# Order of GpSimd's work around the second routing of a mixture-of-experts kernel: weights spread first, gathers of two units ahead of the fifth single's adding, columns ahead of the sixth's

## The chip, the cores and the metric

The kernel runs on one core of a Trainium2 chip. The metric is the device time of one execution in microseconds (us), the median of several. The core has five engines that run side by side and meet at semaphores: TensorE (PE; its weight loads are PEld), VectorE (DVE), ScalarE (ACT), GpSimd (POOL) and SyncE (SP). DMAs are issued by SyncE, ScalarE and GpSimd; all of them run on the same 16 DMA engines. An engine works through its own instructions in their written order: an instruction that waits holds up all that stand behind it on that engine.

## The reference, cut to what matters

`x` is 64 x 64 tokens of 256 numbers. Every token goes to 2 of 8 experts, each of three layers (256 to 512, 512 to 512, 512 to 256), and the weighted sum is added to the token:

```
xn   = rms_w * x * rsqrt(mean(x*x) + 1e-6)
gate = xn @ wg_W + wg_b + (cond @ gg_W + gg_b)
w, i = top_k(softmax(gate), 2)               # cw: the two weights at their experts, else 0
h1   = relu(x @ W1[e] + b1[e])
h2   = relu(h1 @ W2[e] + b2[e])
out  = x + sum over e of cw[e] * (h2 @ W3[e] + b3[e])
```

## The kernel before

Tokens are sorted to their experts, so that only chosen pairs are computed: 4096 tokens x 2 = 8192 pairs. A tile is up to 128 pairs of one expert. For each tile GpSimd does three kinds of DMA with an index per row: a gather of the tokens' rows of x (line 859, into `xg`, `big` or `xgE`), a gather of their routing weights, the "columns" (line 859 too, into `cg`), and at the end an adding of the tile's results onto the rows of `out` in memory (line 1347). An adding reads rows and writes them back, so each unit's adding waits until that of the unit before has landed.

There are two routings. The first covers a quarter of the tokens (`pA`) and fills seven single tiles, units 0 to 6, of which each has an expert of its own: "the fifth single" is unit 4, "the sixth" unit 5. Their indices are `idxA`, their weights lie in memory in `cwdA`. While TensorE works on the singles, the second routing (`pB`, the generator `rest()`, advanced step by step by `routing()`) sorts all that is left: VectorE makes lists, TensorE turns them into a table (line 628), VectorE makes the indices `idxR` of the table (lines 787 and 788). The routing weights of all tokens are worked out by `weights()` on VectorE (lines 433 to 435) and put in place and stored in memory, in `cwdR`, by `spread()` on GpSimd (lines 439 to 442).

From unit 7 on (`F` = 7) a unit is up to four tiles of one expert, and the layers are computed by seven half-size products instead of eight (the classes `Fast` for the first two layers and `Wide` for the third). Unit 7's rows are gathered into `big` and turned by TensorE (line 932). The rows of unit 8 are gathered into `xgE`, and of later units into the two by turns; SyncE regroups them through memory (`stow`, line 898, and `shuffle`, line 905), and VectorE transposes them in blocks (line 914). The copies of x to `out` for the other three quarters of the tokens (`fill`, line 1427) are issued by SyncE too, two before unit 6 and two in unit 6 behind the shuffle of unit 8.

The order is written out by hand (`manual_schedule`): each engine's queue holds its instructions as the program is written. The main program around the change is:

- `head_step(u)` for units 0 to 5: layer 1 of u, layer 3 of u - 1, `give(u - 1)` (VectorE scales the results, line 1346, GpSimd adds them, line 1347), a step of the routing, layer 2 of u. `head_step(5)` gives unit 4, and in it the last step of `rest()` makes the index and gathers unit 7 (`gather_unit(F)`).
- `step(6)`: gathers unit 8, copies and spreads the weights (line 1444 and `spread`), then layer 1 of unit 6, layer 3 and `give` of unit 5, then `gather_cw(7)`, the four gathers of unit 7's columns.
- `step_fast(7)`: gathers unit 9's rows and unit 8's columns; VectorE copies each tile's own column out of `cg` (`scales`, line 1007), then sums products of layer 2 (`c11`, line 1157; in the next step `c22`, line 1163, and `c12`, line 1160); ScalarE scales the biases by the columns (line 1024). `give(6)` comes here.

At a switch in the program ("tail") the later units take one of several written orders, by the data. Each DMA of GpSimd also takes one of eight semaphores in turn, and does not start before the DMA that had the same semaphore, the eighth before it, has landed.

## Time and profile before

| | |
|---|---|
| median of 3 runs | 455.2 us (455.04 to 457.39) |
| the profiled execution | 455.39 us, of it the span 453.7 us |
| busy: TensorE, VectorE, ScalarE, GpSimd | 442.7, 359.2, 259.9, 272.6 us |
| mean granted clock of TensorE | 0.988 |
| moved by DMA | 71.72 MB, 158 GB/s on average |

A row of the timeline gives the start in us from the start of the span, the length, the engine, the line of the kernel, the operation, what it writes and reads (without buffer numbers), how many instructions are merged, and in brackets how long the engine stood idle before and what the wait was put down to. Starts of matmuls are pipelined and their ends are modelled, so the time from start to start is surer than the length. A row of the stretches gives the stretch, its length, the busy time (and number) of PE, PEld, DVE, ACT and POOL, the granted clock of TensorE as a share of full speed, the mean busy share of the DMA engines, and GB/s. "DMA to landing" is the time from the issue of a DMA to its end, least, median and most.

### The profile page before, as it was taken

What the parts mean: (1) busy time and instruction counts of PE and PEld (TensorE: products, weight loads), DVE (VectorE), ACT (ScalarE), POOL (GpSimd) and SP (SyncE); (2) the same over time, 40 slices, a digit from 0 to 9 for tenths busy, and PEclk for the clock granted to TensorE, in tenths of its full rate; (3) what the DMA queues carried; (4) which work ended last, traced back from release to release, by engine and by line L of the source; (5) the groups of instructions that cost most, each with busy time, mean ns of one, the idle gap of its engine ahead of it and who ended that gap; (6) DMA issues with size and microseconds to landing.
All of it is one profiled execution on the core that took longest, in us unless ns stands there. A gap on an engine that the chain in (4) does not pass through costs nothing.

```text
span 453.7 us, 9412 instructions
## 1 busy us (share of the span) xinstructions
PE 442.7 (98%) x3058; PEld 413.8 (91%) x3058; DVE 359.2 (79%) x974; ACT 259.9 (57%) x626; POOL 272.6 (60%) x238
## 2 busy tenths in 40 slices
PE   9999999997999999999999999999999999999994
PEld 7689999786989888989999899999999999999984
DVE  5789996458797979888899788778878888779851
ACT  6865643436464466555565565664764755666642
POOL 5356323868785755648375764864863875766242
PEclk9899999998999999999999999999999999999998
DMA  8799999396776655554655563563663665455213
GB/s 292 296 355 380 367 376 346 104 290 172 190 133 165 110 142 114 116 111 93 167 90 102 124 131 79 130 146 73 124 130 83 111 148 118 115 116 104 23 20 38
DMA packets 71567, 71.72 MB, mean 158 GB/s; under 512 B 35215, under 2 KB 60914, under 8 KB 71124
## 3 DMA queue, kind: packets, MB, share of 16 engines
q1 hardware_dynamic: 48944, 42.51, 29.9%
q0 software_dynamic: 14960, 17.50, 23.3%
q10 hardware_dynamic: 7604, 11.02, 7.7%
q8 instruction: 26, 0.43, 0.4%
q14 instruction: 33, 0.27, 0.2%
HBM read 55.42 MB, written 20.25 MB: 167 GB/s over the span
## 4 chain that ended last, share of the span: by engine, by line
PE 82%; DMA 5%; issue 4%; POOL 4%; DVE 3%; POOLq 1%; ACT 0%; SPq 0%; DVEq 0%; ACTq 0%
PE pb L1145 51%; PE pb L1247 18%; PE pb L1046 4%; PE pb L1315 3%; PE pb L1036 2%; DMA big<-in_x_dram 2%; POOL out_dram L1347 2%; DMA w3r<-in_L_cond_W_dram 1%; DMA cg<-cwdR,idxR 1%; PE pb L258 1%; POOL xgE L859 1%; POOL big L859 1%; DVE xT L914 0%; PE pb L628 0%; DVE big L1122 0%
## 5 line engine op out<-in xcount | busy, mean ns | idle before, releaser
L1347 POOL DMA_INDIRECT out_dram<-ys,idxR x58 | 100.2, 1728 | 89.5 <-DVE ys L1346 75.2
L1145 PE MATMUL pb<-hid,big 128*128 128x256 f32 (+7 forms) x456 | 84.5, 329 | 0.0
L1166 ACT ACTIVATE hid<-hid,bb 128x256 f32<-128x256 f32 (+12 forms) x154 | 73.5, 527 | 14.0 <-DVE hid L1160 13.5
L859 POOL DMA_INDIRECT cg<-cwdR,idxR x60 | 65.2, 1087 | 20.4 <-issue 18.1
L1145 PEld LDWEIGHTS pb<-hid,big 128*128 128x128 f32 x456 | 71.2, 191 | 4.4 <-ACT hid L1166 0.8
L1154 ACT COPY big<-pb 128x512 f32<-128x512 f32 (+7 forms) x57 | 27.5, 482 | 67.6 <-PE pb L1145 50.5
L1145 PE MATMUL pb<-mixB,big 128*128 128x256 f32 (+7 forms) x304 | 58.1, 335 | 2.5 <-DVE hid L1163 2.5
L1145 PE MATMUL pb<-hotA,big 128*128 128x256 f32 (+7 forms) x304 | 56.2, 328 | 0.0
L1145 PEld LDWEIGHTS pb<-mixB,big 128*128 128x128 f32 x304 | 49.4, 194 | 6.5 <-DVE hid L1163 2.8
L1145 PEld LDWEIGHTS pb<-hotA,big 128*128 128x128 f32 x304 | 47.1, 191 | 2.3
L1145 PE MATMUL pb<-mixX,iotx 128*128 128x256 f32 (+7 forms) x228 | 47.0, 329 | 0.0
L859 POOL DMA_INDIRECT xgE<-in_x_dram,idxR x33 | 35.7, 1083 | 10.1 <-issue 8.8
L1154 ACT COPY q1s<-pb 128x512 f32<-128x512 f32 (+7 forms) x57 | 27.2, 476 | 22.1 <-PE pb L1145 20.8
L1145 PEld LDWEIGHTS pb<-mixX,iotx 128*128 128x128 f32 x228 | 36.7, 191 | 3.1 <-issue 0.8
L1268 DVE TENSOR_TENSOR ys<-pb,big 128x256 f32<-128x256 f32 (+1 forms) x54 | 19.2, 355 | 24.8 <-PE pb L1247 19.0
L859 POOL DMA_INDIRECT big<-in_x_dram,idxR x27 | 29.2, 1080 | 8.2 <-issue 7.6
L1024 ACT ACTIVATE bc<-b_sb,cw 128x256 f32 x60 | 26.6, 499 | 9.7 <-DVE cw L1007 8.9
L914 DVE STREAM_TRANSPOSE xT<-gTs 128x256 f32<-128x256 f32 x56 | 30.0, 644 | 2.8 <-DMA gTs<-scr 2.8
L1145 PE MATMUL pb<-xT,w1r 128*128 128x256 f32 (+7 forms) x152 | 31.3, 329 | 0.0
L1166 ACT ACTIVATE hid<-pb,bb 128x256 f32<-128x256 f32 (+7 forms) x76 | 27.7, 417 | 2.4 <-PE pb L1145 1.8
L1256 ACT COPY big<-pb 128x256 f32<-128x256 f32 (+1 forms) x54 | 17.0, 314 | 20.8 <-PE pb L1247 20.7
L1247 PE MATMUL pb<-w3r,hid 128*128 128x128 f32 x216 | 27.2, 275 | 0.0
(347 smaller groups left out, 920.3 us busy)
## 6 DMA issues: line engine op xcount, KB each, us to landing
w2a<-in_L_cond_W_dram SPq DMA_DIRECT2D x8, 1024.0 KB, 11.2
w3r<-in_L_cond_W_dram ACTq DMA_DIRECT2D x11, 512.0 KB, 4.3
w1r<-in_L_cond_W_dram SPq DMA_DIRECT2D x10, 512.0 KB, 11.1
w1r<-in_L_cond_W_dram ACTq DMA_DIRECT2D x10, 512.0 KB, 3.8
w3r<-in_L_cond_W_dram SPq DMA_DIRECT2D x9, 512.0 KB, 11.5
gTs<-scr SPq DMA_DIRECT2D x8, 512.0 KB, 4.4
out_dram<-in_x_dram SPq DMA_DIRECT2D x4, 768.0 KB, 8.3
scr<-xgE SPq DMA_DIRECT2D x6, 512.0 KB, 4.0
```

Source lines behind the costliest of these rows:

```text
L859: return nc.gpsimd.indirect_dma_start(out=dst, out_offset=None, in_=src, in_offset=bass.IndirectOffsetOnAxis(ap=index(b), axis=0), bounds_ ...
L914: V.transpose(xT[:, :, s0 + k, :].rearrange("p c (b k) -> p k c b", b=SQ), shs[:, s0 + k].rearrange("p k (a c) -> p k c a", a=SQ),)
L1024: nc.scalar.mul(bc, b3e, cw)
L1046: nc.tensor.matmul(ph, lhsT=w2[:, m, ts(n, P)], rhs=hid[0][:, m, 0:BT], start=(m == 0), stop=(m == MC - 1))
L1145: nc.tensor.matmul(bank[:, ts(n, self.w)], lhsT=w[:, c, ts(n, P)], rhs=x[:, c], start=new and n == 0 and c == 0, stop=n == HB - 1 and c == ...
L1154: nc.scalar.copy(self.q[(1, 6, 5).index(k)], self.tall(self.X if k == 5 else self.U))
L1166: nc.scalar.activation(out, src, AF.Relu, bias=ww[self.u][1][:, self.l, n : n + 1])
L1247: nc.tensor.matmul(bank[:, ts(j, H // 2)], lhsT=a[:, c, ts(j, P)], rhs=b[:, c], start=new and j == 0 and c == 0, stop=j == self.n - 1 and ...
L1256: nc.scalar.copy(self.q[(1, 6, 5).index(k)], self.X if k == 5 else self.U)
L1268: V.tensor_tensor(self.y(j, i), src, self.q[q].rearrange("p (k h) -> p k h", k=self.n), ALU.add)
L1315: nc.tensor.matmul(sums(u, k)[0 : cols.stop - cols.start], lhsT=hid[1][:, n, cols], rhs=w3[:, n, :], start=(i == 0), stop=(i == MC - 1),)
L1347: add = nc.gpsimd.indirect_dma_start(out=orows, out_offset=bass.IndirectOffsetOnAxis(ap=index(b)[0:n], axis=0), in_=y[0:n], in_offset=None ...
```

## The change

Three things move on GpSimd, and nothing else does: the orders of the other engines stay as they were.

The spread of the weights (the copy of the first part's weights, three operations and the DMA to `cwdR`) leaves `step(6)` and stands in `rest()` right behind `weights()`, ahead of the index and of the gathers of unit 7. The addings of units 4 and 5 leave `give`, which now only notes them in `owed`; `pay()` issues them one by one: unit 4's in `step(6)` behind the gathers of unit 8, unit 5's behind the columns of unit 7.

```diff
         pB.weights()
+        nc.gpsimd.tensor_copy(cw8B[:, 0:NA, :], pA.cw8)
+        pB.spread(cwdR, cw8B, 0)
         yield
         table()
...
         if u not in given:
             given[u] = 0
-            adds.append([])
+            if not F - 3 <= u < F - 1:
+                adds.append([])
...
             given[u] += 1
+            if F - 3 <= u < F - 1:
+                owed.append((b, y[0:n]))
+            else:
+                add_rows(b, y[0:n])
...
+    owed = []
+
+    def pay():
+        adds.append([])
+        add_rows(*owed.pop(0))
+
+    def add_rows(b, y):
...
         if u == F - 1:
             gather_unit(F + 1)
-            nc.gpsimd.tensor_copy(cw8B[:, 0:NA, :], pA.cw8)
-            pB.spread(cwdR, cw8B, 0)
+            pay()
             layer1(u)
...
             give(u - 1)
             gather_cw(F)
+            pay()
```

`add_rows` holds the adding as it stood in `give`, with the same waits.

The queue of GpSimd where the fifth single's adding stood, before. The names are those of the program: `out_0_dram<-ys_193` are the addings of units 2 and 3, `out_0_dram<-xg_1_208` that of unit 4, `big_89` the gathers of unit 7, `xgE_184` those of unit 8, `cw8B_138` the weights being spread:

```order
L1347 DMA out_0_dram<-ys_193,idxA_130 4096x256 x2
L1347 DMA out_0_dram<-xg_1_208,idxA_130 4096x256
L859 DMA big_89<-in_x_dram,idxR_131 128x256 x4
L859 DMA xgE_184<-in_x_dram,idxR_131 128x256 x4
L1444 COPY cw8B_138<-cw8A_162 128x64
L439 TENSOR_TENSOR cw8B_138<-ohB_173,denB_169 128x192
L440 TENSOR_TENSOR wB_172<-ohB_173,d2B_170 128x192
L441 TENSOR_TENSOR cw8B_138<-cw8B_138,wB_172 128x192
L442 DMA cwdR_58<-cw8B_138 128x256
```

The same place of the same queue now (line numbers are those of the changed file, in which 859 is 861, 1347 is 1366 and 1444 is 785):

```order
L1366 DMA out_0_dram<-ys_193,idxA_130 4096x256 x2
L785 COPY cw8B_138<-cw8A_162 128x64
L439 TENSOR_TENSOR cw8B_138<-ohB_173,denB_169 128x192
L440 TENSOR_TENSOR wB_172<-ohB_173,d2B_170 128x192
L441 TENSOR_TENSOR cw8B_138<-cw8B_138,wB_172 128x192
L442 DMA cwdR_58<-cw8B_138 128x256
L861 DMA big_89<-in_x_dram,idxR_131 128x256 x4
L861 DMA xgE_184<-in_x_dram,idxR_131 128x256 x4
L1366 DMA out_0_dram<-xg_1_208,idxA_130 4096x256
```

The spread has moved ahead of the eight gathers, and unit 4's adding from ahead of them to behind them.

Right behind this in GpSimd's queue, before. `xg_2_209` and `xg_0_207` hold the results of units 5 and 6, the two times four gathers into `cg_185` are the columns of units 7 and 8, and those into `big_89` the rows of unit 9:

```order
L1347 DMA out_0_dram<-xg_2_209,idxA_130 4096x256
L859 DMA cg_185<-cwdR_58,idxR_131 128x8 x4
L859 DMA big_89<-in_x_dram,idxR_131 128x256 x4
L859 DMA cg_185<-cwdR_58,idxR_131 128x8 x4
L1347 DMA out_0_dram<-xg_0_207,idxA_130 4096x256
```

And now:

```order
L861 DMA cg_185<-cwdR_58,idxR_131 128x8 x4
L1366 DMA out_0_dram<-xg_2_209,idxA_130 4096x256
L861 DMA big_89<-in_x_dram,idxR_131 128x256 x4
L861 DMA cg_185<-cwdR_58,idxR_131 128x8 x4
L1366 DMA out_0_dram<-xg_0_207,idxA_130 4096x256
```

Unit 5's adding has moved behind unit 7's columns; the rest stands as it did.

## The prediction

> **What bounds the kernel now.** I read the page first, for the engine that is nearly always busy.

> ```profile
> span 453.7 us, 9412 instructions
> PE 442.7 (98%) x3058; PEld 413.8 (91%) x3058; DVE 359.2 (79%) x974; ACT 259.9 (57%) x626; POOL 272.6 (60%) x238
> ```

> TensorE is the bound, so GpSimd's order is worth only what it costs TensorE in waits. The stretches of the trace (length, then the busy time of each engine, the granted clock, the DMA share) say where those are.

> ```profile
> 102.00:104.00 2.00, 0.52 (x3) 0.12 (x1) 0.86 (x4) 1.15 (x3) 1.59 (x2) 1.00 1.04 355
> 104.00:106.00 2.00, 1.13 (x3) 0.95 (x4) 2.00 (x6) 1.84 (x5) 1.50 (x2) 0.69 0.46 140
> 106.00:108.00 2.00, 2.00 (x6) 1.57 (x5) 1.96 (x4) 1.24 (x3) 1.70 (x2) 0.50 0.31 59
> 108.00:110.00 2.00, 2.00 (x10) 1.77 (x9) 1.74 (x4) 1.23 (x3) 1.50 (x2) 0.96 0.85 207
> ...
> 110.00:150.00 40.00, 40.00 (x241) 36.70 (x241) 33.13 (x73) 20.91 (x43) 29.52 (x23) 1.00 0.65 151
> 150.00:240.00 90.00, 89.85 (x539) 82.10 (x538) 76.30 (x175) 51.24 (x109) 54.41 (x43) 1.00 0.56 124
> 262.00:435.00 173.00, 173.00 (x1298) 170.34 (x1296) 141.38 (x382) 107.60 (x276) 107.01 (x80) 1.00 0.50 106
> ```

> The hole is at 102 to 105 us, and behind it the clock is 0.69 and 0.50. From 110 us on TensorE is full, so time won before that should come through to the end. The two timelines of the hole, TensorE's and then VectorE's (start, length, idle before it):

> ```profile
> 99.77 1.89 PE L1145 MATMUL pb<-hid,big 128*128 128x256 f32 x8
> 101.50 1.03 PE L1145 MATMUL pb<-mixX,iotx 128*128 128x256 f32 x4
> 104.87 3.60 PE L1145 MATMUL pb<-mixB,big 128*128 128x256 f32 x8 [2.35 <-DVE hid L1163]
> 108.31 1.03 PE L1145 MATMUL pb<-xT,w1r 128*128 128x256 f32 x4
> ```

> ```profile
> 97.27 2.11 DVE L914 STREAM_TRANSPOSE xT<-gTs 128x256 f32<-128x256 f32 x4 [2.79 <-DMA gTs<-scr]
> 99.41 0.43 DVE L1128 TENSOR_TENSOR mixX<-xT 128x256 f32<-128x256 f32 x1
> ...
> 103.45 0.15 DVE L1007 COPY cw<-cg 128x1 f32 x1 [0.18 <-DMA cg<-cwdR,idxR]
> 103.53 0.69 DVE L1157 TENSOR_TENSOR hid<-pb,big 128x512 f32<-128x512 f32 x1
> 104.14 0.68 DVE L1163 TENSOR_TENSOR hid<-pb,big 128x512 f32<-128x512 f32 x1
> ```

> TensorE waits for unit 7's sum at L1163, which needs nothing from the routing weights; it merely stands on VectorE behind the four copies of L1007, which wait for the gathered columns cg. Those come late from GpSimd:

> ```profile
> 66.88 1.56 POOL L1347 DMA_INDIRECT out_dram<-ys,idxA  x1 [7.18 <-DVE big L777]
> 74.35 1.55 POOL L1347 DMA_INDIRECT out_dram<-xg,idxA  x1 [5.91 <-DMA w3r<-in_L_cond_W_dram]
> 76.20 1.08 POOL L859 DMA_INDIRECT big<-in_x_dram,idxR  x1 [0.30 <-issue]
> ...
> 85.54 1.16 POOL L859 DMA_INDIRECT xgE<-in_x_dram,idxR  x1 [0.30 <-issue]
> 86.71 0.24 POOL L1444 COPY cw8B<-cw8A 128x64 f32<-128x64 f32 x1
> ...
> 89.17 0.63 POOL L442 DMA_DIRECT2D cwdR<-cw8B  x1 [0.30 <-POOL cw8B L441]
> 90.10 1.95 POOL L1347 DMA_INDIRECT out_dram<-xg,idxA  x1 [0.31 <-issue]
> 93.69 1.07 POOL L859 DMA_INDIRECT cg<-cwdR,idxR  x1 [1.64 <-DMA cwdR<-cw8B]
> ...
> 97.69 1.00 POOL L859 DMA_INDIRECT cg<-cwdR,idxR  x1 [0.30 <-issue]
> ```

> The adding at 74.35 stood 5.91 us until the adding before it had landed. (The row names a load of weights, but in the code it waits only for its own rows, which VectorE had written before, and for that adding; the releaser in the row is inferred.) Everything behind it stood too, though the indices were there:

> ```profile
> 67.65 0.18 DVE L435 TENSOR_TENSOR d2B<-d2B,denB 128x24 f32<-128x24 f32 x1
> ...
> 69.98 0.23 DVE L788 SCALAR_TENSOR_TENSOR idxR<-pb,sa 128x70 int32<-128x70 f32 x1
> ```

> **The change part by part.** No engine gets other work; nothing is added or removed but places in GpSimd's queue.

> *Spread first.* Its last input is ready at 67.65 + 0.18 = 67.83 us, the adding ahead of it leaves GpSimd at 66.88 + 1.56 = 68.44. Four operations and one DMA took from 86.70 to 89.80, 3.10 us; now they end at 71.54. They fill the wait of 5.91 us, so they cost TensorE nothing; without that cover they would cost the gathers 3.10 us.

> *Gathers of two units ahead of the fifth adding.* The first starts at 71.54 + 0.31 = 71.85 instead of 76.20, 4.35 earlier (index ready at 70.21). Eight take 86.70 - 76.20 = 10.50 us and end at 82.35. TensorE wants unit 7's rows here:

> ```profile
> 80.29 0.92 PE L932 MATMUL pb<-ident,big 128*128 128x128 f32 x4
> ...
> 82.46 0.27 PE L932 MATMUL pb<-ident,big 128*128 128x128 f32 x1
> 83.06 0.62 PE L932 MATMUL pb<-ident,big 128*128 128x128 f32 x3 [0.33 <-DMA big<-in_x_dram,idxR]
> 83.52 1.03 PE L1145 MATMUL pb<-xT,w1r 128*128 128x256 f32 x4
> ```

> The second set of four would end at 82.46 + 0.92 = 83.38 instead of 83.06 + 0.62 = 83.68: 0.30 us to win. Landing times bound the risk (columns; rows; the plain copies x to out; and one row of the DMA issues, its last column the landing):

> ```profile
> DMA to landing us min/median/max: 2.2/4.2/7.5
> ...
> DMA to landing us min/median/max: 2.8/4.5/6.2
> ...
> DMA to landing us min/median/max: 7.1/8.3/9.6
> ...
> w3r<-in_L_cond_W_dram SPq DMA_DIRECT2D x3, 512.0 KB, 10.9
> ```

> The second gather, now at 71.85 + 1.30 = 73.15, must land by 80.29, and the fourth, at 75.75, by about 82.5. Even the slowest gather of rows, 6.2 us, gives 79.35 and 81.95. The eight semaphores hold nobody: the seventh gather, at 71.85 + 6 x 1.30 = 79.65, waits for the adding of 66.88, which had landed by 74.35, and the eighth, 1.30 later, for the weights' write, which leaves GpSimd at 71.54 and needed 93.69 - 89.80 = 3.89 us to land. I take no wait; the ends are 2.8 and 7.5 us, and at 7.5 TensorE loses 0.4 and keeps the second wait.

> [...]

> ```profile
> 73.77 0.69 DVE L1092 COPY big<-w2a 128x1024 f32 x1
> 74.37 0.43 DVE L1094 COPY big<-w2a 128x512 f32 x1
> ```

> The gather at 76.20, beside other work of VectorE, took 1.08 us, 0.08 over the 1.00 at 97.69; no gather stands beside these copies in the trace. I take 0.1 for all of them; the far end is a gather held for both copies, 1.12 us, which would use up the 0.94 us of room (80.29 - 79.35). [...]

> *Fifth adding, then columns, then sixth adding.* The fifth goes at 82.35 + 0.31 = 82.66 and leaves at 84.21. The columns start at 84.52, not 93.69: 9.17 us earlier, the fourth at 88.52. Slowest landing, 7.5: 96.0 us. The sixth adding waits for the fifth to land, 84.21 + 5.91 = 90.12, about where it was (90.10); only unit 9's gathers queue behind it, at some 92.4 instead of 99.00 us. Nobody on TensorE waits for an adding here.

> *SyncE's queue.* Its order stays; the regrouping of unit 8's rows waits for their gathers, so with it everything behind moves up by 4.35 us, these too:

> ```profile
> 92.95 1.16 SPq L1427 DMA_DIRECT2D out_dram<-in_x_dram x2
> ```

> They start at 88.60, the crowd that delayed the columns goes with them, and three of the four columns are now issued before it.

> *What is late next.* L914 can start at 97.27 - 4.35 = 92.92 if VectorE is free; even where it stood, the copies come at 99.9 and are done at 100.5, and the sums end 1.29 us later (103.53 to 104.82), at 101.8. TensorE asks for L1163 when the four matmuls of 101.50 are through: 101.50 + 0.87 = 102.37 (the same form runs 0.86 or 0.87 from start to start). So the columns may land as late as 100.9, 4.9 us after their slowest case, and the wait goes wholly: 104.87 - 102.37 = 2.50 us.

> *The clock.* The eight matmuls behind the hole take 108.31 - 104.87 = 3.44 us, eight of the same size before it 101.50 - 99.77 = 1.73. Without the hole I expect the clock to stay at 1.00: 1.71 us. [...]

> **The sum:** 0.30 + 2.50 + 1.71 = 4.51 us. The profiled execution took 455.39 us (its span 453.7 and 1.7 around it), 0.2 over the median of 455.2. I forecast 455.2 - 4.5 = 450.7 us; the 0.1 us of the gathers comes out of their room.

> **The rivals.** *The crowd moves with the columns.* They land with the last of the copies, now also delayed by the fifth adding and unit 9's gathers; a wait of up to 1 us stays on L1163. For it: those gathers now run into the crowd. Against it: the copies' slowest landing gives 88.60 + 9.6 = 98.2, below 100.9. It gives 451.7, or 453.4 if the clock falls too.

> *The clock falls anyway*, for another reason than the hole: 455.2 - 2.8 = 452.4. Against it: it is 1.00 before the hole and after 110. [...]

> *Given back later.* A faster TensorE meets another wait, say the switch into the tail near 150 us, where 0.15 us idle stand now. Up to 455.2; the full rows from 110 us speak against it.

> *It does nothing:* the columns' landing hangs on the crowd alone and ends at 103.4 again: 455.2.

> *Slower: unit 7's rows come late.* They are issued into the fullest DMA stretch, behind an adding and the weights' write. Every us after 80.29 is one of TensorE's, and once it waits as long as the hole did the clock costs another 1.71. With the gains of 4.21 left, it is even from a wait of 2.50, a landing 9.6 us after the issue, as of the slowest copy. At the 10.9 of the w3r loads the wait is 3.76: 3.76 + 1.71 - 4.21 = 1.26, 456.5 us; slower by 0.5% from a landing in 12 us.

> **How the numbers follow.** Forecast 0.74, crowd 0.10, clock 0.05, given back 0.05, nothing 0.03, late rows 0.03. The forecast's own range is 449.8 to 451.5 (wait ends of 0.4 and 0.3, and the spread of the executions); the clock case and the better half of the crowd bring it to 452.9, with some 0.85 inside. A measurement of this kernel can tell about 0.5%, 2.3 us, from no change. Below 452.9: forecast, clock, half the crowd, a part of given back, 0.86; slower 0.03; the rest 0.11.

> **What would show it.** Right: spread at 68 to 72 on GpSimd, first gather near 72, columns near 84.5, L1007 without a wait, TensorE without idle time at 102 and the clock 1.00 there, the same lengths from 110 on. Wrong: idle time before L932 near 80, a wait of L1163 or L914 that TensorE feels, a low clock without a hole, or new holes after 110.

## The result, and the profile after

The changed kernel takes 449.21 us (median of 6 runs, 449.06 to 449.97), the kernel before beside it 455.14 (6 runs, 454.83 to 457.39): a ratio of 0.9864, 95% interval 0.9844 to 0.9885, or 5.2 to 7.1 us faster. The forecast was 450.7, with a range from 449.8: the direction was right, and the gain was larger than the range allowed. The profiled execution took 449.12 us, 6.27 less than that of before. In two groups of experiments the kernel before itself took 476 to 477 us, with waits between the engines all over the program, and nothing is concluded from those kernels.

The page after, its first lines:

```profile
span 447.3 us, 9411 instructions
PE 438.9 (98%) x3058; PEld 411.8 (92%) x3058; DVE 359.5 (80%) x974; ACT 259.1 (58%) x626; POOL 273.8 (61%) x238
```

Every engine's busy time is within 1.2 us of before's, but for TensorE's and its weight loads', 3.8 and 2.0 us less. The stretches where the hole was, and one of 173 us behind the switch into the tail:

```profile
100.00:102.00 2.00, 2.00 (x11) 1.77 (x10) 1.91 (x4) 1.17 (x3) 1.70 (x2) 1.00 0.53 175
102.00:104.00 2.00, 2.00 (x11) 1.77 (x10) 1.38 (x4) 1.40 (x4) 1.39 (x3) 1.00 0.06 9
...
255.00:428.00 173.00, 173.00 (x1296) 170.30 (x1296) 141.30 (x382) 107.56 (x276) 107.37 (x80) 1.00 0.51 106
```

No hole, a clock of 1.00, and the stretch of 173 us that ran full before runs full again. GpSimd's timeline after:

```profile
66.25 1.57 POOL L1366 DMA_INDIRECT out_dram<-ys,idxA  x1 [7.29 <-DVE big L778]
67.25 0.82 POOL L785 COPY cw8B<-cw8A 128x64 f32<-128x64 f32 x1
67.46 1.24 POOL L439 TENSOR_TENSOR cw8B<-ohB,denB 128x192 f32<-128x192 f32 x1
...
70.29 0.65 POOL L442 DMA_DIRECT2D cwdR<-cw8B  x1 [0.30 <-POOL cw8B L441]
71.25 1.10 POOL L861 DMA_INDIRECT big<-in_x_dram,idxR  x1 [0.30 <-DMA w3r<-in_L_cond_W_dram]
...
73.97 1.42 POOL L861 DMA_INDIRECT big<-in_x_dram,idxR  x1 [0.30 <-issue]
75.69 1.52 POOL L861 DMA_INDIRECT big<-in_x_dram,idxR  x1 [0.30 <-issue]
...
82.78 1.61 POOL L1366 DMA_INDIRECT out_dram<-xg,idxA  x1 [0.30 <-issue]
84.69 1.04 POOL L861 DMA_INDIRECT cg<-cwdR,idxR  x1 [0.31 <-issue]
...
90.00 2.10 POOL L1366 DMA_INDIRECT out_dram<-xg,idxA  x1 [0.30 <-issue]
92.40 1.26 POOL L861 DMA_INDIRECT big<-in_x_dram,idxR  x1 [0.30 <-PE pb L1147]
```

The wait of 5.91 us is filled, the columns start at 84.69 instead of 93.69. VectorE's timeline where L914 (now 916), the copies (now 1009) and L1163 (now 1165) stand:

```profile
92.73 2.09 DVE L916 STREAM_TRANSPOSE xT<-gTs 128x256 f32<-128x256 f32 x4
...
95.20 0.21 DVE L1009 COPY cw<-cg 128x1 f32 x2
95.59 0.28 DVE L1009 COPY cw<-cg 128x1 f32 x2 [0.18 <-issue]
...
97.45 0.69 DVE L1165 TENSOR_TENSOR hid<-pb,big 128x512 f32<-128x512 f32 x1 [0.95 <-PE pb L1147]
```

The copies wait for no DMA now, and at L1165 it is VectorE that waits for TensorE. TensorE's timeline at unit 7's rows and at the former hole:

```profile
79.45 0.64 PE L934 MATMUL pb<-ident,big 128*128 128x128 f32 x4
79.93 0.60 PE L1317 MATMUL pb<-w3r,hid 128*128 128x256 f32 x2
...
81.34 0.63 PE L934 MATMUL pb<-ident,big 128*128 128x128 f32 x4
81.80 1.03 PE L1147 MATMUL pb<-xT,w1r 128*128 128x256 f32 x4
...
99.77 1.03 PE L1147 MATMUL pb<-mixX,iotx 128*128 128x256 f32 x4
100.64 1.89 PE L1147 MATMUL pb<-mixB,big 128*128 128x256 f32 x8
102.36 0.81 PE L1147 MATMUL pb<-xT,w1r 128*128 128x256 f32 x3
```

Set against before's rows, by the start of the same instructions on TensorE, the 6.4 us of difference between the spans come at four places:

| place | before minus after, us |
|---|---|
| start of the kernel, ahead of everything changed | 0.79 |
| unit 7's rows: four matmuls, layer work, four matmuls | 0.93 |
| hole (2.50) and half clock (3.44 - 1.72) | 4.23 |
| short waits for ScalarE near 157 us | 0.39 |

The first and the last are not the change's. The first is a clock that was low in before's profiled execution and not in the changed kernel's; before, then after, the stretch from 20 us:

```profile
20.00:22.00 2.00, 2.00 (x10) 1.32 (x7) 1.20 (x7) 1.19 (x3) 1.90 (x4) 0.50 0.51 146
```

```profile
20.00:22.00 2.00, 1.64 (x16) 1.39 (x13) 1.83 (x8) 1.07 (x2) 1.89 (x4) 1.00 0.68 144
```

Nothing before 66 us was changed, and the low clock turns up at this place in three later profiles that hold the change's own parts (the third part left out, the hole put back, one of the two repeats of the change; granted clocks over the whole span 0.993, 0.994 and 0.993) and not in the others (0.995 to 0.999, and 0.993 with the sixth adding alone, where it fell behind the hole). The last is not the change's either. The stretch of products around it took TensorE 10.55 us in before and 10.16 in the changed kernel, but 9.89 to 10.25 in the nine later profiles, and 9.89 to 10.14 in those of them that are before with the sixth adding moved or with products in the hole. So 5.2 of the 6.3 us belong to the change: 0.93 + 4.23 = 5.16.

### The profile page after: what moved, and what is told of

The parts are those of the page before. It is cut to its first block, busy times and chain, and to the rows that moved or that the text cites. A ratio compares the mean times of both kernels' runs of the same rounds, so it can differ in the third digit from the quotient of the medians.

```text
span 447.3 us, 9411 instructions
## 1 busy us (share of the span) xinstructions
PE 438.9 (98%) x3058; PEld 411.8 (92%) x3058; DVE 359.5 (80%) x974; ACT 259.1 (58%) x626; POOL 273.8 (61%) x238
## 4 chain that ended last, share of the span: by engine, by line
PE 91%; DMA 3%; DVE 2%; issue 1%; POOLq 1%; POOL 1%; SPq 0%; DVEq 0%
PE pb L1147 57%; PE pb L1249 19%; PE pb L1048 6%; PE pb L1317 3%; PE pb L1038 3%; DMA big<-in_x_dram 2%; PE pb L628 1%; POOL out_dram L1366 1%; DMA xg<-in_x_dram,idxA 1%; DVE xT L916 0%; PE pb L924 0%; POOLq L1693 0%; PE pb L1294 0%; POOLq L1782 0%; PE pb L258 0%
## 5 line engine op out<-in xcount | busy, mean ns | idle before, releaser
L1366 POOL DMA_INDIRECT out_dram<-ys,idxR x58 | 98.7, 1701 | 90.4 <-DVE ys L1349 75.8
L1147 PE MATMUL pb<-hid,big 128*128 128x256 f32 (+7 forms) x456 | 84.5, 329 | 0.0
L1147 PEld LDWEIGHTS pb<-hid,big 128*128 128x128 f32 x456 | 71.2, 191 | 4.4 <-ACT hid L1168 0.8
L1147 PE MATMUL pb<-mixB,big 128*128 128x256 f32 (+7 forms) x304 | 56.3, 328 | 0.2 <-DVE hid L1165 0.2
L1147 PE MATMUL pb<-hotA,big 128*128 128x256 f32 (+7 forms) x304 | 56.2, 328 | 0.0
L1147 PEld LDWEIGHTS pb<-mixB,big 128*128 128x128 f32 x304 | 48.4, 191 | 3.4 <-ACT bc L1026 0.5
L1147 PEld LDWEIGHTS pb<-hotA,big 128*128 128x128 f32 x304 | 47.1, 191 | 2.3
L1147 PE MATMUL pb<-mixX,iotx 128*128 128x256 f32 (+7 forms) x228 | 46.9, 329 | 0.0
L861 POOL DMA_INDIRECT xgE<-in_x_dram,idxR x33 | 37.2, 1127 | 10.1 <-issue 8.5
L1147 PEld LDWEIGHTS pb<-mixX,iotx 128*128 128x128 f32 x228 | 36.8, 191 | 2.9 <-issue 0.8
L861 POOL DMA_INDIRECT big<-in_x_dram,idxR x27 | 30.5, 1129 | 8.2 <-issue 7.3
L1147 PE MATMUL pb<-xT,w1r 128*128 128x256 f32 (+7 forms) x152 | 31.3, 329 | 0.0
## 6 DMA issues: line engine op xcount, KB each, us to landing
w3r<-in_L_cond_W_dram ACTq DMA_DIRECT2D x11, 512.0 KB, 3.8
w1r<-in_L_cond_W_dram SPq DMA_DIRECT2D x10, 512.0 KB, 11.0
w1r<-in_L_cond_W_dram ACTq DMA_DIRECT2D x10, 512.0 KB, 3.7
w3r<-in_L_cond_W_dram SPq DMA_DIRECT2D x9, 512.0 KB, 12.0
gTs<-scr SPq DMA_DIRECT2D x8, 512.0 KB, 4.6
scr<-xgE SPq DMA_DIRECT2D x6, 512.0 KB, 3.9
```

Of the source, the lines that this page charges most:

```text
L861: return nc.gpsimd.indirect_dma_start(out=dst, out_offset=None, in_=src, in_offset=bass.IndirectOffsetOnAxis(ap=index(b), axis=0), bounds_ ...
L1147: nc.tensor.matmul(bank[:, ts(n, self.w)], lhsT=w[:, c, ts(n, P)], rhs=x[:, c], start=new and n == 0 and c == 0, stop=n == HB - 1 and c == ...
L1366: add = nc.gpsimd.indirect_dma_start(out=orows, out_offset=bass.IndirectOffsetOnAxis(ap=index(b)[0 : y.shape[0]], axis=0), in_=y, in_offse ...
```

## The experiments

Theories stood against each other for the gain: mine, that the columns' earlier issue closes the hole and the clock then holds; and rivals, that the gain comes from elsewhere (unit 7's rows, the crowd of DMAs, a clock that falls with or without the hole). The parts were tried alone, the hole was filled and it was put back.

### The kernels on which nothing can be read

Eight runs, of five kernels, stood beside a kernel before of 476 to 477 us. Their diffs show the main lines, with "..." for others. The spread alone, twice (the two lines moved into `rest()`, the addings left in `give`):

```diff
...
         pB.weights()
+        nc.gpsimd.tensor_copy(cw8B[:, 0:NA, :], pA.cw8)
+        pB.spread(cwdR, cw8B, 0)
         yield
...
```

> The spread alone is moved ahead of the index; both addings stay where they were. Theory (columns late, hole, half clock): the spread lies in the wait of 5.9 us before the fifth adding and costs nothing; rows of units 7 and 8 come as before (first gather near 76 us), so the 0.9 us at unit 7's transposes stay lost; the columns start near 89.2 instead of 93.7 us and land by 100.7 at the worst, before 100.9, so the hole (2.5) and the half clock (1.7) go: 455.1 - 4.2 = 450.9 us. Rival (the columns' landing hangs on the crowd of plain copies, which here does not move): landing stays near 103, hole and clock stay, 455 us. Rival (the 1.4 us beyond the forecast come with the earlier columns): 449.8 us or less.

> The spread alone moved, once more, on another day of the chips: in the first trial the kernel before itself took 477 us, with waits at every step between the engines, so that nothing could be read. Theory: rows as before (first gather near 76 us), columns from 89.2 us, landed by 100.7: hole and half clock go, the 0.9 us at unit 7's transposes stay lost: 450.9 us. Rival (crowd holds the columns): 455 us. Rival (what came beyond the forecast comes with the earlier columns): 449.8 us or less.

Measured: 478.6 us, ratio 1.0056 (1.0018 to 1.0094), and 478.44, 1.0046 (1.0006 to 1.0086).

The fifth adding alone behind the gathers (`owed` for unit F - 3 only, the spread left behind it), twice:

```diff
...
             gather_unit(F + 1)
+            pay()
             nc.gpsimd.tensor_copy(cw8B[:, 0:NA, :], pA.cw8)
...
```

> Only the fifth single's adding is moved, behind the gathers of unit 8; the spread stays behind it, the sixth's adding ahead of the columns. Theory: first gather near 70.5 us, so unit 7's transposes wait for nothing (0.9 us won); the spread ends near 86 us, the sixth adding waits for the fifth to land and leaves near 90.7, the columns start near 91 and the crowd of plain copies moves up with the rows to about 87.4, so that the columns land near 99, in time: hole and clock go too, 455.1 - 0.9 - 4.2 = 450.0 us. Rival (columns land 7 us after their start as in the kernel before): fourth in at 101 to 102, a hole of up to 1 us and perhaps the half clock: 451 to 453 us.

> Only the fifth single's adding moved, once more. Theory: first gather near 70.5 us, no wait at unit 7's transposes (0.9 us won); columns from about 91 us, the crowd earlier with the rows, landed near 99: hole and clock go too: 450.0 us. Rival (columns land 7 us and more after their start, at 101 to 102): a hole of up to 1 us, perhaps with the half clock: 451 to 453 us.

Measured: 474.27 us, 0.9985 (0.994 to 1.003), and 473.65, 0.9954 (0.9923 to 0.9986).

The sixth adding alone behind the columns (`owed` for unit F - 2 only):

```diff
...
             gather_cw(F)
+            pay()
...
```

> Only the sixth single's adding is moved, behind unit 7's columns. Theory: the columns still wait for the weights' write to land, near 93 us, rows and crowd stay as before, so nearly nothing is won: 455.1 us, or a little less if the columns land faster without the adding queued ahead of them on the DMA engines. Rival (the adding, 2 us on GpSimd and some 5 us to land, is what holds the columns): columns start at 90 to 91 and land by 100, hole and clock go: 450.9 us.

Measured: 474.37 us, 0.984 (0.9734 to 0.9945).

The kernel before with the hole filled by products that nobody reads, twice:

```diff
+            if u == F + 1:
+                for _ in range(11):
+                    nc.tensor.matmul(PB[6][:, 0:H], lhsT=ident, rhs=b3_sb[:, 0], start=True, stop=True)
```

> The kernel before, with eleven needless products of 256 columns put on TensorE where it stood idle at 102.4 us (into a bank that nobody uses then; results unchanged). They take 11 x 0.216 = 2.4 us, so the wait for the columns is as long as before but TensorE is busy in it. Theory (the idle stretch is what halves the clock): the clock stays at 1.00 there and 1.7 us are won: 453.4 us. Rival (the clock falls there for another reason): 0.50 in the profile near 106 us and 455.1 us. If the products run past the wait they cost up to 0.1 us.

> The kernel before with eleven needless products of 256 columns in TensorE's idle stretch at 102.4 us, once more. Theory (the idle stretch halves the clock): clock 1.00 there, 1.7 us won: 453.4 us. Rival (the clock falls for another reason): 0.50 near 106 us and 455.1 us.

Measured: 478.65 us, 1.007 (1.0032 to 1.0108), and 480.68, 1.0091 (1.0047 to 1.0134).

The changed kernel with the hole put back by reductions on VectorE that nobody reads:

```diff
...
+            if u == F + 1:
+                for wide in (2048, 2048, 1376):
+                    V.tensor_reduce(idle, b3_sb.rearrange("p e h -> p (e h)")[:, 0:wide], AX.X, ALU.add)
             before.c22()
```

> The changed kernel, in which VectorE sums the biases three times to no use (some 5.9 us) ahead of unit 7's sum that TensorE waited for; rows, columns and addings stay as in the changed kernel, so only TensorE's hole comes back, some 2.4 us long. Theory: 2.4 us for the hole and 1.7 for the half clock behind it: 449.2 + 4.1 = 453.3 us, and the rest of the gain (1.8 us: unit 7's transposes 0.9, the rest elsewhere) stays. [...] Rival (the gain had little to do with the hole): 449.2 to 450 us.

Measured: 483.07 us, 1.0005 (0.9924 to 1.0086). Its TensorE shows why none of these times speaks of the change, at a place where before's TensorE shows no wait:

```profile
93.32 2.08 PE L1147 MATMUL pb<-xT,w1r 128*128 128x256 f32 x4 [9.50 <-DVE xT L935]
```

That is 9.50 us for a copy on VectorE, far from the edit, and more than all that is at stake. The waits of TensorE that the view lists come to 17 to 25 us in the eight profiles, and to 4.6 in before's. What disturbed these runs was not settled, and the changed kernel itself was not run beside them, so whether it gains anything there is not shown. All later runs stood beside a kernel before of 455.4 to 456.0 us.

### The change again

> The changed kernel itself, beside the kernel before on the same chip, as a measure for the other trials. Where the kernel before takes 455 us: 449.2 us, 5.9 less. Where it takes 476 us, as in the two trials before this one, with TensorE's semaphores coming in late while the DMA engines are full: theory (the columns and the rows arrive earlier, whatever else waits): still some 4 us less; rival (there the hole at 102 us is filled by other waits, so nothing is left to win): 476 us.

> The changed kernel once more, on the chip of these trials. Theory: 5.2 us less than the kernel before (0.9 at unit 7's transposes, 2.5 for the hole, 1.7 for the half clock where it falls there), give or take 0.5 by how often the half clock falls in the kernel before. Rival (a real further gain of 0.7): 5.9 us less, again.

No edit. Measured: 450.34 us, 0.9887 (0.9854 to 0.9921), and 449.44, 0.9869 (0.984 to 0.9899). Beside the first result of 0.9864 the gain stands: 1.1 to 1.4% three times. In both profiles the rows cost nothing again, and the hole and the low clock behind it are gone (0.93 and 4.22 or 4.23 us less than in before's profile).

### The spread alone

The diff is the first above.

> The spread alone moved ahead of the index, the addings where they were; third trial, since in the first two the kernel before itself took 476 us. Theory: rows as before (first gather near 76 us), columns from 89.2 us, landed by 100.7: hole (2.5) and half clock (1.7) go, the 0.9 us at unit 7's transposes stay lost: 4.2 less than the kernel before, 451 us. Rival (the crowd of plain copies, which stays in its place here, holds the columns): no gain, 455 us. Rival (what came beyond the forecast comes with the earlier columns): 5.5 less or more.

Measured: 451.6 us, 0.9903 (0.9871 to 0.9935). The hole and the low clock went, with the columns issued from 89.88 us; TensorE, and ahead of it the fifth adding on GpSimd:

```profile
75.22 1.63 POOL L1349 DMA_INDIRECT out_dram<-xg,idxA  x1 [3.79 <-DVE big L1096]
...
89.88 1.03 POOL L861 DMA_INDIRECT cg<-cwdR,idxR  x1 [0.31 <-issue]
```

```profile
80.86 0.39 PE L934 MATMUL pb<-ident,big 128*128 128x128 f32 x1 [1.13 <-DMA big<-in_x_dram,idxR]
...
102.45 1.03 PE L1147 MATMUL pb<-mixX,iotx 128*128 128x256 f32 x4
103.31 1.89 PE L1147 MATMUL pb<-mixB,big 128*128 128x256 f32 x8
```

The products of L1147 follow without a break, so the spread alone suffices for the hole. But at unit 7's rows TensorE stood 1.13 us at the first product alone, where before shows 0.33 in all: the gathers still come behind the fifth adding, which was later here (75.22) than in before's profile (74.35).

### The fifth adding alone

The diff is the second above.

> Only the fifth single's adding moved, behind the gathers; third trial. Theory: first gather near 70.5 us, no wait at unit 7's transposes (0.9 us won), columns from about 91 us and landed near 99 with the crowd earlier too: hole and clock go: 5.1 less than the kernel before, 450 us. Rival (columns land 7 us and more after their start, at 101 to 102): a hole of up to 1 us, perhaps with the half clock: 2 to 4 less.

Measured: 450.44 us, 0.9872 (0.9845 to 0.99). The rows cost nothing, the columns go out from 89.48 us, and there is no hole. So this part alone does both things, and its time is as good as that of the whole change within the intervals. It pays at another place: the spread now runs beside VectorE's sums of layer 2. GpSimd, VectorE and TensorE there:

```profile
83.98 0.97 POOL L439 TENSOR_TENSOR cw8B<-ohB,denB 128x192 f32<-128x192 f32 x1
84.61 0.96 POOL L440 TENSOR_TENSOR wB<-ohB,d2B 128x192 f32<-128x192 f32 x1
```

```profile
84.01 1.84 DVE L1128 TENSOR_TENSOR mixX<-xT,mixX 128x256 f32<-128x256 f32 x1
...
86.71 0.41 DVE L1128 TENSOR_TENSOR mixX<-xT,mixX 128x256 f32<-128x256 f32 x1
```

```profile
85.91 1.13 PE L1145 MATMUL pb<-mixX,iotx 128*128 128x256 f32 x4 [0.82 <-DVE mixX L1128]
```

The same operation of VectorE takes 0.41 us when GpSimd computes nothing and 1.84 beside the spread, and TensorE waits 0.82 us for it (1.12 by the starts). That is what the spread's early place saves in this profile; in the times it does not show.

### The sixth adding alone, and all but it

The first is the third diff above; the second is the changed kernel with only unit F - 3 in `owed` and without the second `pay()`.

> Only the sixth single's adding moved behind unit 7's columns; second trial. Theory: the columns wait for the weights' write to land as before, near 93 us; they land at most 2 us earlier without the adding ahead of them on the DMA engines: 0 to 2 us less than the kernel before. Rival (this adding is what holds the columns): hole and clock go, 4 us less.

> The change without its third part: spread first, fifth adding behind the gathers, but the sixth adding ahead of the columns as before. Theory: the sixth waits until the fifth has landed, 90.1 us, the columns start at 92.3; with the crowd moved up to 88.6 they land near 99 to 101, just in time or up to 0.5 us late: 0 to 0.5 us more than the changed kernel. Rival (the third part carries the gain): the hole of 2.4 us stays, 2.4 to 4.1 more than the changed kernel.

Measured: alone 456.63 us, 1.002 (0.9996 to 1.0043), no gain; all but it 450.18, 0.9885 (0.9855 to 0.9915), beside 0.9869 for the change. Alone it can do nothing, for the columns then wait for the write of the weights instead; GpSimd, then VectorE's last copy and TensorE:

```profile
75.88 1.77 POOL L1364 DMA_INDIRECT out_dram<-xg,idxA  x1 [7.09 <-DMA w3r<-in_L_cond_W_dram]
...
95.75 1.32 POOL L859 DMA_INDIRECT cg<-cwdR,idxR  x1 [3.97 <-DMA cwdR<-cw8B]
```

```profile
106.24 0.15 DVE L1007 COPY cw<-cg 128x1 f32 x1 [0.29 <-DMA cg<-cwdR,idxR]
```

```profile
81.45 0.39 PE L932 MATMUL pb<-ident,big 128*128 128x128 f32 x1 [1.54 <-DMA big<-in_x_dram,idxR]
...
107.66 3.59 PE L1145 MATMUL pb<-mixB,big 128*128 128x256 f32 x8 [3.15 <-DVE hid L1163]
```

The hole is even longer, 3.15 us, the clock falls behind it (eight matmuls in 3.59 us), and at the rows the first product alone waits 1.54 us. In the change the third part is worth 0.3 us at the hole by the profiles; the times, 0.7 us apart with overlapping intervals, don't tell it from nothing.

### The hole filled, and put back

The diffs are those with products and with reductions above; a third kernel has 5 products instead of 11.

> The kernel before with eleven needless products of 256 columns in TensorE's idle stretch at 102.4 us; third trial. Theory (the idle stretch halves the clock): clock 1.00 there, 1.7 us less than the kernel before, 453.4 us. Rival (the clock falls for another reason): 0.50 near 106 us and no gain.

> The kernel before with five needless products in the hole, not eleven: each ran as two passes, so that eleven took 4.7 us and outlasted the hole by some 2 us. Five take 10 x 0.216 = 2.2 us. Theory (the idle stretch brings the half clock, but only in executions in which it falls badly to the clock's windows of 3.4 us): clock 1.00 at 106 us in the profile, and the median falls by the share of the executions that had the half clock, 0.5 to 1.7 us: 453.7 to 455. Rival (the half clock there is as good as sure): 1.7 less. Rival (it has another cause): no gain.

> The changed kernel with three needless sums on VectorE (some 5.9 us) ahead of unit 7's sum, so that TensorE's hole of some 2.4 us comes back and nothing else; second trial. Theory: 2.4 for the hole and 1.7 for the half clock: 4.1 more than the changed kernel, 453.3 us. Rival (the hole alone does not halve the clock): 2.4 more, 451.6 us. Rival (the gain had little to do with the hole): 449.2 to 450 us.

Measured: 11 products 456.23 us, 1.0013 (0.999 to 1.0037); 5 products 454.79, 0.9985 (0.9966 to 1.0004); hole put back 453.24, 0.9942 (0.9915 to 0.9969). TensorE with 11 products, with 5, and with the hole put back:

```profile
104.07 4.91 PE L1551 MATMUL pb<-b_sb,ident 128*128 128x256 f32 x22
108.81 1.89 PE L1145 MATMUL pb<-mixB,big 128*128 128x256 f32 x8
```

```profile
103.35 2.32 PE L1551 MATMUL pb<-b_sb,ident 128*128 128x256 f32 x10
106.14 1.99 PE L1145 MATMUL pb<-mixB,big 128*128 128x256 f32 x8 [0.46 <-DVE hid L1163]
```

```profile
104.65 1.99 PE L1147 MATMUL pb<-mixB,big 128*128 128x256 f32 x8 [2.50 <-DVE hid L1165]
106.48 1.03 PE L1147 MATMUL pb<-xT,w1r 128*128 128x256 f32 x4
```

With 11 products the miss was mine: each runs as two matmuls, 22 in 4.74 us, and they outlast the hole they should fill; the clock behind them stays at 1.00. With 5 the hole is filled but for 0.46 us, the clock stays at 1.00, and the time falls by 0.7 us by the ratio, with an interval from 1.6 faster to 0.2 slower. The third is the surprise: the hole is back with 2.50 us, longer than before's 2.35, and the eight matmuls behind it take 106.48 - 104.65 = 1.83 us, at full clock. So idle time of this length was followed by the half clock in one profile (before) and not in another; the steps of the clock, further down, tell the two apart. Put back, the hole costs 2.5 to 3.3 us by the ratios (0.9942 less 0.9887 or 0.9869, of 455.5 us): the hole itself and 0 to 0.8 us of clock, on the average of the executions, an estimate since the intervals of the two overlap; the granted clocks further down put it at the upper end or above.

## Why the prediction was right, and where it was wrong

**The bound, the hole, the queue: right.** TensorE is full from 110 us on and passes the gain to the end. The steps on GpSimd came near to what was worked out: spread at an end of 70.94 (forecast 71.54, with the start of the kernel 0.8 us earlier), eighth gather's end at 82.48 (82.35), fifth adding 82.78 (82.66), columns from 84.69 (84.52), sixth adding 90.00 (90.12), unit 9's gathers 92.40 (92.4). That they meet within 0.2 us from the eighth gather on is partly luck: the gathers began 0.6 us early and took 11.23 us instead of 10.50. The hole went wholly, 2.50 us: L1165 waits for TensorE now.

**The clock: right in the pair, and for a reason that the prediction did not have.** 1.72 us were won between the two profiles, 1.71 forecast. The prediction went by the hole in before; the hole put back was as long and left the clock at 1.00. The clock records in the traces say what differs. In the two traces of the pair the times from one change of the clock to the next are whole multiples of 3.413 us (in before 13.653, 3.413, 81.920, 3.413 and 341.333 us, in the changed kernel 440.319), so there the clock changed only on a grid of that step. Below are the steps of this grid around the hole in before, with the sixth adding alone, and with the hole put back; the first number behind the length is TensorE's busy time:

```profile
101.34:104.75 3.41, 1.18 (x6) 0.70 (x4) 1.61 (x6) 1.99 (x5) 2.55 (x3) 1.00 0.97 328
104.75:108.16 3.41, 3.29 (x8) 2.66 (x9) 3.32 (x9) 2.65 (x6) 2.80 (x3) 0.50 0.34 80
```

```profile
104.48:107.90 3.42, 0.27 (x2) 0.24 (x2) 1.82 (x6) 1.63 (x4) 2.75 (x3) 1.00 0.71 171
```

```profile
100.65:104.07 3.42, 1.50 (x7) 0.97 (x6) 3.38 (x3) 0.00 (x0) 2.81 (x3) 1.00 0.17 35
104.07:107.48 3.41, 2.83 (x13) 2.52 (x14) 3.41 (x8) 2.03 (x5) 2.50 (x4) 1.00 0.96 217
```

The steps with 1.18 and 0.27 us of work were followed by one at half clock. The hole put back lies across a boundary of the grid, so that its emptiest step still held 1.50 us of work, and the clock held. The ends of the kernels fit: behind a step with 1.44 us of work (before, from 446.08 us) the clock fell, behind one with 1.71 (the changed kernel, from 439.46) it held. The grid lay differently in each of these executions: near the hole a step began at 101.34 us in before, 101.54 in the changed kernel, 104.48 with the sixth adding alone and 100.65 with the hole put back. That would let the same hole cost the clock in one and not in another, an estimate from these few steps. This does not account for the low clock near 20 us, which in before came behind a step with 3.25 us of work; that stays open.

How often the hole costs the clock can be estimated from the granted clock of every execution. (1 - clock) times the span is 3.2 us on the average of the 69 executions of kernels with the hole (before, sixth adding alone, hole put back), and 1.9 on that of the 58 of kernels without it (the change, spread alone, fifth alone, all but the sixth, both with products). Both hold the low clock at other places, which all these kernels share. The difference of 1.3 us, with a standard error of 0.2, is an estimate of what the clock behind the hole costs on average, where the prediction had 1.71.

**The rows: wrong, and this is the step that put the time out of the range.** The prediction had "0.30 us to win" at unit 7's transposes. The pair shows 0.93, and other profiles more. With 0.93 in its place the sum would be 5.14 us, the forecast 450.1 and the low end of its range 449.2, so that the measured 449.21 would lie just inside. Two things failed. First, the price of a set that waits for nothing. I took the 0.92 us of the first set's row, and the 0.33 us that the second set's matmuls were shown waiting. TensorE's weight loads, which run ahead of its matmuls (in the changed kernel those of L934 start at 79.35 us, the matmuls at 79.45), tell another story; before, then after:

```profile
80.29 0.73 PEld L932 LDWEIGHTS pb<-ident,big 128*128 128x128 f32 x4
...
83.06 0.43 PEld L932 LDWEIGHTS pb<-ident,big 128*128 128x128 f32 x3 [0.62 <-DMA big<-in_x_dram,idxR]
```

```profile
79.35 0.55 PEld L934 LDWEIGHTS pb<-ident,big 128*128 128x128 f32 x4
```

The loads of the second set waited 0.62 us for the rows, and the product behind it came 83.52 - 82.46 = 1.06 us after the set's start; now it is 81.80 - 81.34 = 0.46, which wins 0.60. The first set's loads were late too (0.73 us for four instead of 0.55): 81.05 - 80.29 = 0.76 us from start to start, now 79.93 - 79.45 = 0.48, which wins 0.28. What held those is not named in the view of waits. So the set that I took for free was itself delayed, and the wait of the matmuls was only the part of the loads' wait that earlier matmuls did not cover.

Second, I took one execution's wait for the kernel's. The fifth adding's start hangs on the landing of the adding before it, and that varies: it landed at 73.57 us in before, 73.96 with 5 products, 75.34 with 11 and 75.10 with the sixth adding alone, and each time the fifth started 0.78 us later. (With the spread alone the trace has no such landing.) The profiled kernels that keep the fifth adding ahead of the gathers (starts in us from each span's own start; the loss by the starts of the same instructions on TensorE, against the changed kernel):

| kernel | fifth adding | first gather | weight loads' waits for rows | lost on TensorE |
|---|---|---|---|---|
| before | 74.35 | 76.20 | 0.6 | 0.93 |
| 5 products in the hole | 74.74 | 77.11 | 1.8 | 1.96 |
| spread alone | 75.22 | 77.16 | 2.4 | 2.57 |
| 11 products in the hole | 76.12 | 77.97 | 2.5 | 2.64 |
| sixth adding alone | 75.88 | 77.95 | 3.3 | 3.42 |

Here each us by which the gathers came later cost TensorE about one. Counted against TensorE's products just ahead of the rows, which in these profiles ran 0.79, 0.75, 0.11, 0.80 and 0.29 us later than in the changed kernel, the first gather starts at 75.41, 76.36, 77.05, 77.17 and 77.66 us. In the six profiles with the fifth adding behind the gathers (the change three times, fifth alone, all but the sixth, hole put back) the loss is 0 within 0.06 us.

None of the edits in the table touches GpSimd's queue between the adding of unit 3 and the fifth, but for the spread alone, which only fills the wait there. So before's profiled execution, the lowest of the five, was a lucky one to read, and the term is 0.9 to 3.4 us by the profiles, not 0.30. Its size in an average execution of before is not shown directly, for the others have no trace. Of the 5.9 us between the medians, 2.50 for the hole and 1.3 for the clock leave some 2.1 for the rows, an estimate; the ratio of the spread alone, which leaves the rows late, lies 0.7 to 1.5 us above those of the change, with overlapping intervals.

**The gathers beside VectorE: the price was wrong, at no cost.** In the changed kernel unit 7's gathers run beside VectorE's copies of the second layer's weights. I took 0.1 us for all; two of them took 1.42 and 1.52 us instead of 1.00, 0.9 in sum. Only the first, at 73.97, ran beside the copies, which stood from 74.58 to 75.62 us; the second, at 75.69, came behind them. So the gather beside the copies took 0.42 us more, and what lengthened the other is not shown. In the first repeat of the change the two took 1.42 and 1.48 us. The far end, a gather held for both copies (1.12 us), was my estimate, and no row here shows it. The 0.9 us came out of the room: TensorE's first set at 79.45 waited for nothing.

**The rivals.** The crowd did move up with the columns (SyncE's copies of x went at 89.31 us instead of 92.95) and delayed nobody, since the copies at 95.20 found their columns. The clock did not fall for another reason: at this place it is 1.00 in all eight profiles whose hole is closed or filled. Unit 7's rows came in time. Nothing was given back later: the full stretches stayed full.

**Which part does it.** The spread or the fifth adding, either alone, takes the hole away; only the fifth adding takes away the wait for the rows; only the spread's early place keeps its operations clear of VectorE's sums; the sixth adding's place is worth 0.3 us at most in the profiles. No kernel tried here beats the change; the fifth adding alone (0.9872) and all but the sixth (0.9885) can't be told from it (0.9864 to 0.9887).

## What to carry to other kernels

The wait that hung on a DMA's landing had no one price here: before's profile shows 0.33 us of it on TensorE's matmuls, and four profiles of near kernels lost 2.0 to 3.4. Where a single profile shows a little of such a wait, profile the kernel twice or set its range by the landing times. On TensorE read the waits of the weight loads, not those of the matmuls alone: here they came within 0.1 to 0.3 us of what was lost. And an engine that stands for a landing (GpSimd, 5.91 us) is the first place to put work that it must do later anyway, best clear of another engine's sums (beside the spread one of VectorE's took 1.84 us instead of 0.41).
